# A graph network's five summing passes: separate PSUM places in place of windows, node values ahead of the pass, and f32 queries

## The chip, the cores and the metric

One core of one Trainium2 chip runs the whole kernel in one launch. The metric is the device time of that core in microseconds (us); lower is better. The kernel before takes 8,166.93 us, the median of 3 runs (8,162.49 to 8,179.8).

## The reference

Four graph layers stand one behind the other, each followed by a residual and a layer norm. There are 6,250 nodes of 128 features and 100,000 edges sorted by destination:

```python
x = _layernorm(x + _L0_gnn_ref(...))   # two GAT layers: softmax over a node's edges of leaky_relu(s[src] + d[dst])
x = _layernorm(x + _L1_gnn_ref(...))   # segment_sum(xw[src] * norm, dst)
x = _layernorm(x + _L2_gnn_ref(...))   # 8 heads: q from x[dst], k and v from a message of x[src], edge type and time
x = _layernorm(x + _L3_gnn_ref(...))   # segment_sum(m[src], dst), then a GRU cell
```

The core of each layer is `segment_sum(values of edges, dst)`: a row of 128 features for each edge, got by its source node, weighted and summed into its destination node. Layer 0 does this twice, the others once. Layer 2 needs the query row of each edge's destination as well, layer 0 the attention term `d[dst]`.

## The kernel before, in words

Nodes lie in NB = 49 blocks of 128. The edges are cut into K = 832 tiles of up to 128 edges, so that all edges of a tile go to nodes of one block. Which block that is depends on the data, so the kernel works it out on the chip (L225 to L251) and keeps it as integers for registers. U = 16 tiles make a group, 48 tiles a chunk (CHUNKS).

A summing pass goes over the 832 tiles. GpSimd (POOL in the profile) gathers 128 source rows for each tile with an indirect DMA (`gather`, L137). A 128 x 128 f32 one-hot `sel` says which edge goes to which node of the block; `selections` (L364 on) makes the one-hots once, in the first pass, stores them in the table SELD, 1 MB for 16 tiles, and loads them in all later passes. TensorE multiplies `sel` with the rows into PSUM, and VectorE adds the product to ACC in SBUF, at the place of the tile's block. There are five such passes: `attention_edges(0)`, `attention_edges(1)` (layer 0), `sum_edges` with table Yt and edge weights (layer 1), the value pass L1013 to L1032 (layer 2), which loads its rows from a table by plain DMAs, and `sum_edges` with table Mt (layer 3).

*Windows* (L402 to L458). Three or four consecutive tiles share one PSUM bank. For each pass step of 6, 8 or 12 tiles TensorE loads registers (L415) with the offset of each tile's block from the first block of its window, a bf16 zero matmul clears the bank (L437), and each tile's matmul adds at its register-held offset (L445). VectorE then adds the whole window of 390 to 512 columns to ACC in one instruction (L453), 1,250 in all.

*attention_edges* (L460 to L559). For each chunk the loop gathers 48 tiles into three row buffers (of 7, 16 tiles each). For each group it gets bf16 row one-hots, the transposed selection, from `row_selections` (L377 to L390): in pass 0 they are made from destination rows loaded by two DMAs (L385, `dlrow`, two buffers) and two VectorE compares (L386), and stored in the table RSELD (L387); in pass 1 they are loaded. One matmul with three bf16 columns per tile brings the node's attention term to the edges (L493), in pass 0 a second one brings the node's time (L496); each value is split in three bf16 parts (`by_step`, L349 on), and a reduce adds them (L501, L503). Then comes a chain of small instructions for the softmax's running maximum over the chunk (L505 to L547: transposes on TensorE, scans on VectorE), ScalarE scales the rows (L556), and the sums follow. The chain of a chunk waits for its gathers (L504), and in TensorE's order before, it begins ahead of all 48 sums of the chunk in front.

*Layer 2* has a node stage that writes a table Qt of queries, each split into three bf16 parts (L787 to L791), and then 208 steps of four tiles, whose order on TensorE is written out by hand (`part`, L841 on). A step's `rows_of` (L817 to L838) loads the query rows of each tile's block (L826, 102 KB) and 128 KB of row one-hots; `keys` (L878 to L906) multiplies messages with the key and value weights (L890, f32), and gets queries to edges with three bf16 matmuls (L892). The value pass afterwards loads 256 KB of values per four tiles (L1025) and multiplies them on GpSimd (L1027).

The scheduler of the framework keeps program order on each engine except where priorities move instructions[...].

Of the kernel before, what the change touches and what calls it, by code (L numbers as in the profile page):

```python
# [20 lines left out]
P = 128  # L21
# [14 lines left out]

WINDOWS = {3: W, 4: D}
MW = max(WINDOWS)
# [12 lines left out]
def kernel(ctx: ExitStack, tc: tile.TileContext, a: dict, out: bass.AP):  # L51
# [27 lines left out]
    RSELD = table("rseld", K // U * P, U * P, BF16)  # L79
    TYR = table("tyr", KR, P, BF16)  # L80
# [5 lines left out]
    Qt = table("qt", NP, 3 * W, BF16)  # L86
# [29 lines left out]

    OFF = const.tile([97, K + 4], I32, name="OFF")
    PLACE = {3: OFF[0:1, 0:K], 4: OFF[64:65, 0:K]}
    QOFF = OFF[32:33, 0:K]
    FIRST = {3: OFF[96:97, 0:K // 3 + 1], 4: OFF[96:97, K // 3 + 1:K // 3 + 1 + K // 4]}  # L120
    zero = const.tile([1, BANK], BF16, name="zero")
    nc.vector.memset(zero, 0.0)
# [20 lines left out]
    with tc.tile_pool(name="prep", bufs=1) as pp, tc.tile_pool(name="prepp", bufs=2, space=PSUM) as pq:  # L143
# [97 lines left out]
        for m, w in WINDOWS.items():  # L241
            n = -(-K // m)
            part = 0 if m == 3 else 64
            steps = bkrow[part:part + 1, 0:n * m].rearrange("o (w s) -> o w s", s=m)
            place = pp.tile([P, K + 4], F32, name="place", bufs=2)[part:part + 1, 0:n * m]
            nc.vector.tensor_sub(place.rearrange("o (w s) -> o w s", s=m), steps,
                                 steps[:, :, 0:1].to_broadcast([1, n, m]))
            nc.vector.tensor_scalar(PLACE[m], place[:, 0:K], float(w), None, op0=OP.mult)
            nc.vector.tensor_scalar(FIRST[m], bkrow[96:97, 0:n * m:m], float(W), None, op0=OP.mult)
# [99 lines left out]
    def by_step(keep, work, psum, rows, name):  # L349
# [7 lines left out]
        t3 = keep.tile([P, K, 3], BF16, name=f"{name}t", bufs=1)  # L357
# [4 lines left out]
        return t3  # L362
# [14 lines left out]
    def row_selections(work, k0, make=False, n=U):  # L377

        rs = work.tile([P, n * P], BF16, name="rsel", bufs=4 if n < U else 2)
        tab = RSELD[k0 // U * P:(k0 // U + 1) * P, k0 % U * P:(k0 % U + n) * P]  # L380
        if make:
            for h in range(2):
                n = U * P // 2
                row = work.tile([P, n], BF16, name="dlrow")
                nc.sync.dma_start(row, flat(DLR, k0 * P + h * n, (0, P), (1, n)))  # L385
                nc.vector.tensor_scalar(rs[:, h * n:(h + 1) * n], row, relid, None, op0=OP.is_equal)  # L386
            last = nc.sync.dma_start(tab, rs)  # L387
        else:
            last = nc.sync.dma_start(rs, tab)
        return rs, name_of(last)  # L390
# [11 lines left out]
    class Windows:  # L402
# [4 lines left out]
        def __init__(self, psum, m, banks, windows):  # L407
            self.m, self.w, self.banks, self.group = m, WINDOWS[m], banks, windows * m
            self.ring = psum.tile([P, banks, BANK], F32, name="ring")
            self.todo = []  # L410
            for t0 in range(0, NB + MW, 14):
                nc.vector.memset(ACC[:, t0:min(NB + MW, t0 + 14), :], 0.0)

        def load(self, to, engine, most):
            _, vals = nc.values_load_multi_w_load_instructions(  # L415
                to, engines=[engine], min_val=0, max_val=most,
                skip_runtime_bounds_check_because="a window has as many places as steps, and blocks are below NB")
            return vals

        def add(self, k, sel, rows, after, fade=None, kept=0):  # L420


            m, w, n = self.m, self.w, rows.shape[-1]
            if k % (U * m) == 0:
                k1 = min(K, k + U * m)
                self.to = self.load(FIRST[m][:, k // m:-(-k1 // m)], ET.DVE, (NB - 1) * W)
            if fade is not None:
                self.fades[k] = fade
            self.todo.append((k, sel, rows, after))
# [3 lines left out]
            ks = range(todo[0][0], k + 1)  # L433
            at = self.load(PLACE[m][:, ks[0]:k + 1], ET.PE, (m - 1) * w)
            wins = sorted({q // m for q in ks})
            for i, v in enumerate(reversed(wins)):
                z = nc.tensor.matmul(self.ring[:, v % self.banks, 0:m * w], zero[:, 0:P], zero[:, 0:m * w],  # L437
                                     start=True, stop=False, skip_group_check=True)
                if i == 0:
                    head = z  # L440
                    first_after(z, [a_ for t in todo for a_ in t[3]])
                else:
                    in_order(z, head)
            for q, sel, rows, _ in todo:
                last = nc.tensor.matmul(self.ring[:, q // m % self.banks, ds(at[q - ks[0]], n)], sel, rows,  # L445
                                 start=False, stop=False, skip_group_check=True)
            for v in wins:
                to = self.to[v % U]
                if v * m in self.fades:
                    a0 = ACCF[:, ds(to, kept)]  # L450
                    nc.vector.tensor_scalar(a0, a0, self.fades.pop(v * m), None, op0=OP.mult)
# [769 lines left out]
```

## Time and profile before

| | |
|---|---|
| median of 3 runs | 8,166.93 us |
| profiled execution | 8,259.27 us, span 8,257.5 us |
| mean granted TensorE clock | 0.644 |
| prep and node tables | 0 to 146 us |
| attention_edges(0) | 146 to 1,698 us |
| attention_edges(1) | 1,760 to 3,222 us |
| sum_edges of layer 1 | 3,345 to 4,588 us |
| node stage of layer 2 | to 4,686 us |
| layer 2, 208 steps | 4,686 to 6,430 us |
| value pass | 6,512 to 6,830 us |
| sum_edges of layer 3 | 6,914 to 8,134 us |

The costliest groups of instructions:

```profile
L445 PE MATMUL ring<-g,sel 128*128 128x128 f32 (+2 forms) x6656 | 1532.7, 388 | 1755.5 <-issue 1723.6
L137 POOL DMA_INDIRECT g<-g,SRCT x1664 | 1573.0, 945 | 1524.8 <-issue 836.9
L453 DVE TENSOR_TENSOR ACC<-ACC,ring 128x512 f32 (+3 forms) x1250 | 755.9, 605 | 3734.0 <-remote 2206.2
L437 PE MATMUL ring<-zero 1*128 1x408 bf16 (+1 forms) x1250 | 446.5, 449 | 963.5 <-DVE ACC L453 564.6
L890 PE MATMUL pk<-Wkv,mT 128*128 128x256 f32 x1664 | 681.7, 499 | 94.2 <-DVE qk L900 49.0
L892 PE MATMUL pq<-qb,rsel 128*128 128x136 bf16 x2496 | 331.1, 250 | 0.0
```

A line gives the source line, the engine and the operation, the tile written and the tiles read, the count, then busy time and mean ns of one, then the idle time of the engine just before such instructions and what ended most of it. An f32 matmul stands in the records twice, with two weight loads (PEld). "issue" is time in which an engine waited for nothing that the profile shows, "remote" a wait whose releaser it can't place. DVE is VectorE, ACT is ScalarE. Engine times overlap, so busy times don't add up to the span.

### The profile page before, as it was taken

How to read it: one execution, taken by the hardware profiler on the slowest of the kernel's cores; microseconds unless marked ns; L12 is line 12 of the kernel's file. 1: busy time of each engine (PE TensorE's matmuls, PEld its weight loads, DVE VectorE, ACT ScalarE, POOL GpSimd, SP SyncE). 2: the span in 40 equal slices, each digit the busy share in tenths (PEclk: the TensorE clock that was granted, in tenths of full speed). 3: DMA queues.
4: the chain of work that ended last, by engine and by line, in shares of the span. 5: the costliest groups of instructions: out<-in, count | busy, mean ns of one | idle time of the engine just before them, and what ended most of it. 6: DMA issues, size and time to landing. Idle time of an engine off the chain costs nothing. (4 is left out here: it accounts for less than half of the span.)

```text
span 8257.5 us, 75556 instructions
## 1 busy us (share of the span) xinstructions
PE 3922.3 (47%) x20491; PEld 2792.2 (34%) x20491; DVE 2618.2 (32%) x5807; ACT 1708.1 (21%) x5176; POOL 4221.7 (51%) x4384
## 2 busy tenths in 40 slices
PE   2244444433334433233333377777777693243436
PEld 1133333322223322222222244444444472132224
DVE  3122222231111114110111666566566654011115
ACT  1112121202211111222222233333333110000001
POOL 2555555435555551656666155455553373666661
PEclk8555555555555555555555688788888796555657
DMA  4333433333333322222332466666666592232321
GB/s 109 93 118 111 120 111 118 94 91 108 96 96 96 98 79 59 78 88 88 96 92 89 133 184 186 179 187 185 181 185 169 193 360 66 70 97 87 98 88 60
DMA packets 737110, 997.93 MB, mean 121 GB/s; under 512 B 151865, under 2 KB 594033, under 8 KB 703425
## 3 DMA queue, kind: packets, MB, share of 16 engines
q1 hardware_dynamic: 588090, 662.03, 25.4%
q0 software_dynamic: 146992, 331.03, 16.2%
q8 instruction: 189, 3.10, 0.2%
q14 instruction: 217, 1.77, 0.1%
q10 hardware_dynamic: 1622, 0.01, 0.0%
HBM read 824.55 MB, written 168.09 MB: 120 GB/s over the span
## 5 line engine op out<-in xcount | busy, mean ns | idle before, releaser
L445 PE MATMUL ring<-g,sel 128*128 128x128 f32 (+2 forms) x6656 | 1532.7, 388 | 1755.5 <-issue 1723.6
L137 POOL DMA_INDIRECT g<-g,SRCT x1664 | 1573.0, 945 | 1524.8 <-issue 836.9
L445 PEld LDWEIGHTS ring<-g,sel 128*128 128x128 f32 x6656 | 1336.8, 288 | 2119.7 <-issue 2119.6
L453 DVE TENSOR_TENSOR ACC<-ACC,ring 128x512 f32 (+3 forms) x1250 | 755.9, 605 | 3734.0 <-remote 2206.2
L137 POOL DMA_INDIRECT xa<-xat,SRCT x832 | 855.4, 1028 | 970.0 <-DVE z L872 582.5
L137 POOL DMA_INDIRECT g<-yt,SRCT x832 | 785.0, 943 | 589.8 <-issue 394.7
L137 POOL DMA_INDIRECT g<-mt,SRCT x832 | 785.0, 944 | 489.6 <-issue 345.5
L437 PE MATMUL ring<-zero 1*128 1x408 bf16 (+1 forms) x1250 | 446.5, 449 | 963.5 <-DVE ACC L453 564.6
L890 PE MATMUL pk<-Wkv,mT 128*128 128x256 f32 x1664 | 681.7, 499 | 94.2 <-DVE qk L900 49.0
L556 ACT ACTIVATE g<-g 128x128 f32<-128x128 f32 x1664 | 521.1, 388 | 186.1 <-issue 125.7
L575 ACT ACTIVATE g<-g,EWT 128x128 f32<-128x128 f32 x832 | 324.9, 400 | 863.9 <-DMA g<-yt,SRCT 767.6
L437 PEld LDWEIGHTS <-zero 1*128 1x128 bf16 x1250 | 106.9, 101 | 1073.6 <-issue 928.1
L890 PEld LDWEIGHTS pk<-Wkv,mT 128*128 128x128 f32 x1664 | 310.1, 232 | 132.2 <-DVE qk L900 62.1
L1027 POOL TENSOR_TENSOR vx<-v,exh 128x512 f32<-128x512 f32 x208 | 214.9, 1064 | 247.5 <-DMA v<-vt 221.2
L892 PE MATMUL pq<-qb,rsel 128*128 128x136 bf16 x2496 | 331.1, 250 | 0.0
L892 PEld LDWEIGHTS <-rsel 128*128 128x128 bf16 x2496 | 251.9, 114 | 177.6 <-issue 72.3
L898 ACT COPY kv<-pk 128x512 f32<-128x512 f32 x416 | 239.8, 600 | 348.1 <-PE pq L892 268.6
L542 ACT ACTIVATE f<-f 1x1 f32<-1x1 f32 x36 | 7.3, 202 | 1361.3 <-DVE f L541 1253.8
L860 PE MATMUL rp<-RT,oty 128*128 128x256 bf16 x832 | 259.8, 312 | 21.8 <-DMA qb<-qt 21.8
L323 ACT COPY aT<-tr 128x512 f32<-128x512 f32 (+1 forms) x13 | 7.3, 560 | 1232.2 <-PE tr L321 1232.2
L861 PE MATMUL rp<-RT,oty 64*128 64x256 bf16 x832 | 257.3, 309 | 0.0
L493 PE MATMUL pdn<-D0t,rsel 128*128 128x3 bf16 x1664 | 101.5, 167 | 321.6 <-issue 212.9
(322 smaller groups left out, 4531.4 us busy)
## 6 DMA issues: line engine op xcount, KB each, us to landing
sel<-seld SPq DMA_DIRECT2D x208, 1024.0 KB
qb<-qt SPq DMA_DIRECT2D x832, 102.0 KB
seld<-sel SPq DMA_DIRECT2D x52, 1024.0 KB
vt<-kv SPq DMA_DIRECT2D x208, 256.0 KB
v<-vt SPq DMA_DIRECT2D x208, 256.0 KB
g<-g,SRCT POOLq DMA_INDIRECT x1664
dlrow<-dlr SPq DMA_DIRECT2D x104, 256.0 KB
rseld<-rsel SPq DMA_DIRECT2D x52, 512.0 KB
```

The source lines that it names most:

```text
L137: return nc.gpsimd.indirect_dma_start(out=dst_tile, out_offset=None, in_=tab, in_offset=bass.IndirectOffsetOnAxis(ap=idx, axis=0))
L437: z = nc.tensor.matmul(self.ring[:, v % self.banks, 0:m * w], zero[:, 0:P], zero[:, 0:m * w], start=True, stop=False, skip_group_check=True)
L445: last = nc.tensor.matmul(self.ring[:, q // m % self.banks, ds(at[q - ks[0]], n)], sel, rows, start=False, stop=False, skip_group_check=True)
L453: add = nc.vector.tensor_add(a0, a0, self.ring[:, v % self.banks, 0:m * w] .rearrange("p (b w) -> p b w", w=w)[:, :, 0:n])
L556: scaled = nc.scalar.activation(g[:, q, 0:D], g[:, q, 0:D], AF.Copy, scale=g[:, q, D:D + 1])
L575: scaled = nc.scalar.activation(g[:, q, :], g[:, q, :], AF.Copy, scale=EWT[:, k0 + q:k0 + q + 1])
L860: part(nc.tensor.matmul(rp[:, q, :], oty[:, o:o + P], RT2, start=True, stop=False), after)
L861: part(nc.tensor.matmul(rp[:, q, :], oty[0:REL, o:o + P], RT3, start=False, stop=True), after)
L890: part(nc.tensor.matmul(pk[:, q - q0, :], mT[:, q, :], Wkv, start=True, stop=True), after)
L892: part(nc.tensor.matmul(pq_[:, q - q0, :], rs[:, o:o + P], qb[:, q, i, :], start=i == 0, stop=i == 2), after)
L898: free += [nc.scalar.copy(kv[:, q0:q0 + 2, :], pk), nc.scalar.copy(qbs[:, k0 % U + q0:k0 % U + q0 + 2, :], pq_[:, :, D:]), nc.vector.tenso ...
L1027: i0 = nc.gpsimd.tensor_mul(vx[:, :, 0:D].rearrange("p q (h d) -> p q h d", h=HD), v.rearrange("p q (h d) -> p q h d", h=HD), exh[:, u0:u0 ...
```

## The change: separate places, an earlier pre-pass, f32 queries

Four things change together.

- `Windows` becomes `Sums`. Each tile has a PSUM place fixed at build time, three or four to a bank. The zero matmul and TensorE's register loads go. VectorE adds each tile's product by itself, 128 to 136 columns, 4,160 adds in all, and loads the 16 places of a group of tiles into its registers at once.
- `attention_edges` brings node values to the edges for all 52 groups before the pass's first sum, with one matmul of six (pass 0) or three (pass 1) columns for each tile; in TensorE's order, a chunk's chain now begins after 36 of the 48 sums of the chunk in front.
- `sum_edges` of layer 1 also makes f32 row one-hots, 1 MB for each group, in a new table RSELF.
- Layer 2 keeps its queries in f32 (68 KB a tile's load instead of 102), loads 256 KB of f32 row one-hots a step, and does one f32 matmul for the queries of a tile. The value pass loads 1 MB of values for 16 tiles at once.

```diff
-    class Windows:
+    class Sums:
...
-            at = self.load(PLACE[m][:, ks[0]:k + 1], ET.PE, (m - 1) * w)
-            wins = sorted({q // m for q in ks})
-            for i, v in enumerate(reversed(wins)):
-                z = nc.tensor.matmul(self.ring[:, v % self.banks, 0:m * w], zero[:, 0:P], zero[:, 0:m * w],
-                                     start=True, stop=False, skip_group_check=True)
...
-            for q, sel, rows, _ in todo:
-                last = nc.tensor.matmul(self.ring[:, q // m % self.banks, ds(at[q - ks[0]], n)], sel, rows,
-                                 start=False, stop=False, skip_group_check=True)
...
+            for q, sel, rows, _, to in todo:
+                n = rows.shape[-1]
+                at = self.ring[:, q // self.m % self.banks, q % self.m * width:q % self.m * width + n]
+                mm = nc.tensor.matmul(at, sel, rows, start=True, stop=True)
...
+                a0 = ACCF[:, ds(to, n)]
+                add = nc.vector.tensor_add(a0, a0, at)
...
+            for k0 in range(0, K, U):
+                rs = row_selections(work, k0, l == 0)
+                c0 = k0 // U % slots * U * 6
+                pd = pdn[:, c0:c0 + U * nv].rearrange("p (t i) -> p t i", i=nv)
+                for q in range(U):
+                    nc.tensor.matmul(pd[:, q, :], rs[:, q * P:(q + 1) * P], DN[:, k0 + q, :], start=True, stop=True)
+                nc.vector.tensor_reduce(DE[:, k0:k0 + U], pd[:, :, 0:3], AX.X, OP.add)
+                if l == 0:
+                    nc.vector.tensor_reduce(TMT[:, k0:k0 + U], pd[:, :, 3:6], AX.X, OP.add)
...
                 sel, made_by = selections(work, k0)
+                if weighted:
+                    made_rows(work, k0, work.tile([P, U * P], F32, name="rself", bufs=2),
+                              RSELF[k0 // U * P:(k0 // U + 1) * P, :])
...
-                for i in range(3):
-                    nc.scalar.copy(q3[:, :g, i, :], qt[:, :g])
-                    if i < 2:
-                        nc.vector.tensor_sub(qt[:, :g], qt[:, :g], q3[:, :g, i, :])
-                nc.sync.dma_start(nodes(Qt)[:, t0:t0 + g, :], q3[:, :g].rearrange("p t i w -> p t (i w)"))
+                nc.sync.dma_start(nodes(Qt)[:, t0:t0 + g, :], qt[:, :g])
...
-                            for i in range(3):
-                                part(nc.tensor.matmul(pq_[:, q - q0, :], rs[:, o:o + P], qb[:, q, i, :],
-                                                      start=i == 0, stop=i == 2), after)
+                            part(nc.tensor.matmul(pq_[:, q - q0, :], rs[:, o:o + P], qb[:, q, :],
+                                                  start=True, stop=True), after)
...
+                v = work.tile([P, U, D], F32, name="v")
+                nc.sync.dma_start(v, Vt[k0 * P:(k0 + U) * P, :].rearrange("(q e) d -> e q d", e=P))
```

The new helper `made_rows` holds the loads, compares and store that `row_selections` had:

```python
def made_rows(work, k0, rs, tab):
    for h in range(2):
        n = U * P // 2
        row = work.tile([P, n], BF16, name="dlrow")
        nc.sync.dma_start(row, flat(DLR, k0 * P + h * n, (0, P), (1, n)))
        nc.vector.tensor_scalar(rs[:, h * n:(h + 1) * n], row, relid, None, op0=OP.is_equal)
    nc.sync.dma_start(tab, rs)
```

## The prediction

> **What bounds the kernel now.** I read the page's busy table and slices, then the stages as windows, then the waits, and last short windows inside the passes.
>
> ```profile
> PE 3922.3 (47%) x20491; PEld 2792.2 (34%) x20491; DVE 2618.2 (32%) x5807; ACT 1708.1 (21%) x5176; POOL 4221.7 (51%) x4384
> PE   2244444433334433233333377777777693243436
> POOL 2555555435555551656666155455553373666661
> PEclk8555555555555555555555688788888796555657
> ```
>
> No engine is busy for much over half of the span. So the limit is a hand-over, and it must be looked for stage by stage. The next view cuts the span into layer 0's two attention passes, layer 1's sums, layer 2's steps, layer 2's value pass and layer 3's sums; columns are PE, PEld, DVE, ACT, POOL busy (count), PE clock, DMA share, GB/s.
>
> ```profile
> 146.00:1698.00 1552.00, 613.75 (x3781) 470.96 (x3780) 388.26 (x841) 280.00 (x1000) 786.77 (x832) 0.54 0.36 107
> 1760.00:3222.00 1462.00, 539.34 (x2897) 406.71 (x2898) 213.73 (x648) 278.38 (x955) 783.32 (x830) 0.56 0.33 95
> 3345.00:4588.00 1243.00, 446.10 (x1874) 328.72 (x1874) 159.70 (x261) 324.88 (x832) 784.97 (x832) 0.58 0.30 90
> 4686.00:6430.00 1744.00, 1281.57 (x6775) 815.39 (x6776) 1028.60 (x2144) 635.89 (x1927) 855.39 (x832) 0.80 0.66 178
> 6512.00:6830.00 318.00, 274.61 (x1943) 225.13 (x1942) 191.56 (x356) 45.73 (x206) 214.90 (x208) 0.95 0.99 336
> 6914.00:8134.00 1220.00, 450.41 (x1872) 333.23 (x1872) 142.23 (x208) 0.00 (x0) 785.04 (x832) 0.59 0.30 90
> ```
>
> Four passes of 832 gathers take 1,220 to 1,552 us. A gather is 0.945 us and starts every 1.248 us when nothing holds it, so 832 need 1,038 us: every pass is above that. The value pass has DMA at 0.99. Layer 2's steps have PE busy 74% at clock 0.80. What holds the gather passes is in the waits:
>
> ```profile
> DVE ACC L453 <- remote: 2206.2, 135, 49.0
> PEld ring L445 <- issue: 2153.2, 1324, 5.1
> PE ring L445 <- issue: 1730.3, 1080, 4.5
> ```
>
> VectorE waits for TensorE, and TensorE's sum matmuls wait 1,730 us for nothing that the profile shows. The short windows show when: two stretches of a pass where POOL has gathered without a pause, one after a pause, and layer 1's end after its last gather.
>
> ```profile
> 168.00:284.00 116.00, 7.39 (x45) 4.71 (x45) 1.50 (x5) 0.00 (x0) 87.66 (x94) 0.50 0.30 71
> 3722.00:3752.00 30.00, 4.76 (x13) 3.43 (x13) 0.29 (x1) 8.83 (x22) 18.87 (x20) 0.55 0.17 46
> 3776.00:3789.00 13.00, 13.00 (x60) 10.11 (x59) 4.86 (x8) 3.26 (x9) 9.89 (x11) 0.59 0.62 209
> 4534.00:4584.00 50.00, 34.71 (x235) 27.62 (x234) 32.51 (x69) 0.00 (x0) 0.00 (x0) 0.84 0.41 137
> ```
>
> Under back-to-back gathers TensorE starts one record per 116/90 = 1.29 us or 30/26 = 1.15 us, weight loads and matmuls alike; after a pause, one per 13/119 = 0.11 us. The first window holds only the 3-column matmuls L493 and L496, so the slow pace isn't the work of register offsets or zero matmuls. So TensorE paces the passes, in the stretches where POOL streams; POOL then fills all row buffers, stands still some 6 us, and TensorE catches up.
>
> [...] TensorE's L415 shows 590 in layer 1. [...]
>
> **The change, part by part**, against the profiled span of 8257.5 (8259.27 for that run; the median of the runs, 8166.93, is 0.989 of it, and savings are scaled so).
>
> *No zero matmuls, no offsets on TensorE.* A tile is two weight loads and two matmuls in the records (f32); the zero matmul adds one of each per four tiles: 4.5 records a tile before, 4 after. In layer 1 POOL's cycle is 32 gathers in 45.9 us, 6 of them standing. Slow tiles cost 4.5 x 1.15 = 5.2 us, fast ones 0.49 (13 us for 119/4.5 = 26 tiles): some 26 tiles are done fast in 12.5 us, the other 6 slowly. Afterwards 0.44 and 4.6 us: 12.5/0.44 = 28.6 fast tiles per pause. With C for the cycle, 28.6 + (C - 12.5)/4.6 = (C - 6)/1.248 gives C = 52.5 us for 37.3 tiles, 1.41 us a tile instead of 1.434: 21 us a pass. The register load of TensorE goes too (104 x 0.59 = 61 us a pass); it runs beside queued matmuls, so I count at most 10 of it. Layer 1 and layer 3: -30 each. Bounds: 0 and -150 (gather pace).
>
> *One VectorE add per tile.* L453's adds took 556 ns at 390 columns and 687 at 512: 1.07 ns a column and 138 fixed, so 284 ns at 136, and six in a row took 4.43 us where durations make 4.1, so 0.05 between: 0.335 x 832 = 279 us a pass instead of about 160. A gather pass has 1,220 or more, so VectorE covers it: 0 there. Queued behind a waiting add are the chain of L501 to L547 and the one-hots; TensorE and ScalarE wait for these. In the value pass cover is gone: 279, plus the products with exh and 52 loads of 16 registers (1.1 us each, half exposed), make about 350 against 318: +30 (0 to +50). The 1 MB loads in place of four of 256 KB move the same bytes: 0.
>
> *Row one-hots for f32 queries, made in layer 1.* 52 times two loads, two is_equal with f32 out and a 1 MB store. is_equal in bf16 took 485 ns for 1024[...]. But the store waits for them, and they are behind the former group's adds, and SP issues the next sel load behind the store. DMA share is 0.30, so bytes are free; I take +25 for the coupling (0 to +60).
>
> *Pre-pass.* In attention_edges all 52 groups of 16 tiles get node values before the first sum; then 112 gathers fill the seven row buffers in 140 us and POOL stands until the first sums. Layer 0: 146 us with TensorE slow, about five groups done; then 47 groups at 4 to 5 us (two loads and a store, 1 MB in all: 3.1 us at 336 GB/s; 16 matmuls under 4 us; take 4.5): 212. Then 720 tiles, 15 chunks. A chunk takes 84 us now; its 48 tiles at layer 1's new pace need 68, and about 6 of the chain's stalls stay, because the chain of the next chunk now sits after 36 of a chunk's 48 sums and no longer ahead of all: 74. With 40 at the end: 146 + 212 + 15 x 74 + 40 = 1,508 instead of 1,552: -44. Layer 1 of the two: groups only load their one-hots (512 KB, 1.6 us) and are about 2.3 us: 146 + 46 x 2.3 + 1,110 + 40 = 1,402 instead of 1,462: -60. Bounds from 60 to 84 a chunk: -250 to +105 each.
>
> *Layer 2.* Node stage: 36 casts of 645 ns and 24 subtractions of 718 go, and alternate between two engines: -25 of 40. Steps: PE per tile at full clock is 0.43 for keys and 3 x 0.06 plus an exposed load, about 0.66; an f32 query is 2 x 0.11 and its heavier load: the same 0.66. Query loads fall from 102 to 68 KB, one-hots rise from 128 to 256 KB per four tiles: even. 0 (-20 to +66; the upper end is a load left exposed at 0.08 x 832).
>
> Sum: layers 0 -104, layer 1 -30 + 25, layer 3 -30, node stage -25, value pass +30: -134, or -132 in the median: 8,035, written 8,040.
>
> **Rivals.**
> (a) The pre-pass is not cheap, slower: POOL has nothing to do from its 112th gather to the pass's first sum, and any time a group takes more is added in full. At 8 us a group in layer 0 (load, compare, store in turn with two row buffers) and 4.6 in layer 1: 47 x 3.5 + 46 x 2.3 = 270 more, 8,305. It decides from about 1.4 us more per group in both (134/93). For it: dlrow has two buffers, and nothing in the trace shows this loop alone. Against it: loads of 256 KB and compares of 485 ns are short, and SP has no other work then.
> (b) TensorE falls below the threshold at which POOL waits for it, much faster: layers 1 and 3 at 1.248 us a tile, 1,083 each with a tail of 45: 1,243 + 1,220 - 2,166 = -297 instead of -35: 7,780; if the chunks follow, lower. For it: 0.44 us fast. Against it: without pauses TensorE stays slow at 4.6 us a tile.
> (c) The f32 query doesn't shorten but lengthens TensorE's share of a step, the part that doesn't do what it says: +66, 8,105. For it: clock 0.80 and PE 74% busy; against: VectorE 59% busy shares the step.
>
> **How the numbers follow.** Chances: forecast (7,930 to 8,140) 0.40; (a), 8,190 to 8,450, 0.31; VectorE's adds delay chain and one-hots by as much, 8,185 to 8,300, 0.08; (b), 7,550 to 7,930, 0.12; (c) 0.09, half of it within 0.2%. A measurement of this kernel can't tell less than 0.2% (16 us) from no change. Faster by over 0.2%: 0.40 + 0.12 + 0.03 = 0.55; within: 0.06; slower: 0.39. Leaving out a tenth at each end gives 7,780 to 8,400; the likeliest case alone, 7,930 to 8,140.
>
> **What would show it.** Right: layer 1 and 3 passes near 1,240 and 1,190 with no L437; a gap of POOL of about 210 and 105 us before the first sums of layer 0's passes, and chunks of 74 us; the value pass with DVE over 0.8 busy; steps still 8.4 us. Wrong: longer gaps (a), passes near 1,080 (b), steps over 8.6 us (c). The prediction fails most easily if the slow pace of TensorE changes with the kind of instruction, since its cause isn't known.

## The result, and the profile after

The changed kernel takes 8,526.81 us (median of 4 runs, 8,514.88 to 8,535.17) against 8,164.71 for the kernel before on the same chip: slower, ratio 1.044 (95% interval 1.042 to 1.046). The forecast was 8,040, faster; the range ended at 8,400.

The busy table and the slices of the changed kernel:

```profile
PE 3471.9 (41%) x17577; PEld 2793.6 (33%) x17577; DVE 3140.4 (37%) x8891; ACT 1652.6 (19%) x5137; POOL 4244.2 (50%) x4384
...
PE   2012233232232233323222347888888574133336
...
POOL 2214455543355655166666435555554263666661
...
PEclk8556555556555555555555668888888686555557
```

TensorE has 2,914 records fewer than before, VectorE 3,084 more, as the change says. What is new is at the left: POOL's third slice is at 1, PE's second at 0, and POOL's slices after it stay lower than before. The groups that answer to those of before:

```profile
L418 PE MATMUL ring<-g,sel 128*128 128x128 f32 (+2 forms) x6656 | 1504.4, 384 | 2814.7 <-issue 1816.6
...
L430 DVE TENSOR_TENSOR ACC<-ACC,ring 128x128 f32 (+3 forms) x4160 | 1200.9, 289 | 3217.8 <-remote 2136.9
...
L865 PE MATMUL pq<-qb,rsel 128*128 128x136 f32 x1664 | 404.9, 333 | 0.0
```

The zero matmuls are gone; TensorE's waits without a cause are not (1,723.6 us before, 1,816.6 now). An add takes 289 ns (284 forecast), 1,201 us in place of 756. The queries now take 1,664 records where bf16 took 2,496. By stage, with the columns that the prediction used (layer 0's two passes, layer 1, layer 2's steps, its value pass, layer 3):

```profile
150.00:1971.00 1821.00, 447.73 (x2678) 387.25 (x2678) 481.49 (x1468) 270.01 (x1000) 791.52 (x832) 0.56 0.31 91
2022.00:3547.00 1525.00, 450.40 (x2679) 394.43 (x2678) 317.86 (x1255) 264.56 (x956) 789.58 (x832) 0.56 0.32 91
3649.00:4890.00 1241.00, 355.08 (x1664) 318.79 (x1664) 303.54 (x935) 319.86 (x832) 800.43 (x832) 0.58 0.49 155
4988.00:6692.00 1704.00, 1313.54 (x6044) 958.07 (x6044) 1080.98 (x2238) 635.37 (x1933) 855.18 (x832) 0.82 0.66 181
6692.00:7078.00 386.00, 254.83 (x1685) 235.78 (x1684) 276.10 (x951) 49.24 (x214) 213.40 (x208) 0.84 0.88 287
7172.00:8389.00 1217.00, 390.31 (x1664) 326.18 (x1664) 238.37 (x832) 0.00 (x0) 785.49 (x832) 0.57 0.30 90
```

To compare like with like I cut both traces at the first gather and the last add of each pass (layer 2: first to last gather; value pass: first to last add):

| us | before | after | difference |
|---|---|---|---|
| layer 0, first pass | 1,555 | 1,821 | +266 |
| layer 0, second pass | 1,487 | 1,524 | +37 |
| layer 1 | 1,223 | 1,241 | +18 |
| node stage of layer 2 | 118 | 97 | -21 |
| layer 2's steps | 1,664 | 1,564 | -100 |
| value pass | 295 | 340 | +45 |
| layer 3 | 1,220 | 1,217 | -3 |

With small differences between the stages that makes the 256 us by which the spans differ (8,513.1 and 8,257.5).

These 256 us are not the 362 by which the two medians differ. The profiled run of the kernel before took 8,259 us, 1.1% more than the 8,161 to 8,180 of the four runs beside the changed kernel, and it is none of those four. Two later runs leave most stages as they were, on a chip where the kernel before takes 8,166: e13 (layers 1 and 3, layer 2) and e14 (layer 0). Measured against them, the changed kernel's differences are:

| us | before, from e13 and e14 | after | difference |
|---|---|---|---|
| layer 0, first pass | 1,539 | 1,821 | +282 |
| layer 0, second pass | 1,470 | 1,524 | +54 |
| layer 1 | 1,218 | 1,241 | +23 |
| node stage of layer 2 | 119 | 97 | -22 |
| layer 2's steps | 1,609 | 1,564 | -45 |
| value pass | 301 | 340 | +39 |
| layer 3 | 1,210 | 1,217 | +7 |

That is 338 us, and with some 15 between the stages it comes near the 362. The same stage differs by up to 15 us from one run to the next on such a chip (the first pass takes 1,552 in e16, whose code there is the same), so differences of that size say nothing.

The first pass of layer 0 is most of it by either table. In the two profiled runs its 266 us are a gap of POOL after the 112th gather of 289 us where 56 stood before (+233), and 40 more in the gathers behind it; its end is 10 shorter. The first four chunks behind the gap take 99 to 103 us each and the later ones 80 to 88, where the kernel before takes 81 to 86. In the second pass the gap grows from 30 to 119 us, while the gathers behind it take 1,168 us in place of 1,224.

**Chips of two kinds showed up**. On some the kernel before takes 7,028 to 7,033 us (e1 to e8, e17), on others 8,159 to 8,259 (e9 to e16, e18), and the first comparison was made on one of the latter. I call them the quick and the slow kind; all ratios are against the kernel before on the same chip. The later runs met two chips of the quick kind and four of the slow; one was met twice and was quick both times. The slow kind has two levels: 8,159 to 8,166 (the first comparison, e13 to e16, e18) and 8,250 to 8,259 (e9 to e12, and the trace of before). They differ in layer 2's steps with bf16 queries, 1,607 to 1,609 us (e13, e14) and 1,664 to 1,668 (the trace of before, e11).

The layer 1 pass of the kernel before on the slow kind, two windows side by side, then the same code on the quick kind (in e1, which leaves that pass alone):

```profile
3800.00:3840.00 40.00, 15.66 (x71) 11.65 (x71) 5.50 (x8) 10.77 (x28) 25.94 (x28) 0.63 0.31 99
3840.00:3880.00 40.00, 7.32 (x19) 4.80 (x18) 1.37 (x2) 11.50 (x29) 27.36 (x30) 0.50 0.26 74
```

```profile
3300.00:3340.00 40.00, 17.91 (x72) 14.00 (x72) 5.50 (x8) 12.41 (x33) 30.25 (x33) 0.66 0.33 106
3340.00:3380.00 40.00, 18.78 (x72) 14.37 (x72) 5.50 (x8) 12.28 (x33) 30.25 (x33) 0.62 0.32 105
```

On the quick kind TensorE does 72 matmul records in each of the two windows and POOL 33 gathers, its full pace; on the slow kind the records fall to 19 once POOL has streamed for a while. (A record is one instruction of TensorE in the trace.) The granted clock is lower there, but by a fifth only, 0.50 in place of 0.63, while the records fall to about a quarter. So the slow pace that the prediction found in the trace goes with the chip, not with the program alone.

### The profile page after: what moved, and what is told of

It reads as the page before. It is cut to its first block, busy times and chain, and to the rows that moved or that the text cites. A ratio compares the mean times of both kernels' runs of the same rounds, so it can differ in the third digit from the quotient of the medians.

```text
span 8513.1 us, 71240 instructions
## 1 busy us (share of the span) xinstructions
PE 3471.9 (41%) x17577; PEld 2793.6 (33%) x17577; DVE 3140.4 (37%) x8891; ACT 1652.6 (19%) x5137; POOL 4244.2 (50%) x4384
## 5 line engine op out<-in xcount | busy, mean ns | idle before, releaser
L418 PE MATMUL ring<-g,sel 128*128 128x128 f32 (+2 forms) x6656 | 1504.4, 384 | 2814.7 <-issue 1816.6
L430 DVE TENSOR_TENSOR ACC<-ACC,ring 128x128 f32 (+3 forms) x4160 | 1200.9, 289 | 3217.8 <-remote 2136.9
L865 PEld LDWEIGHTS pq<-qb,rsel 128*128 128x128 f32 x1664 | 406.3, 244 | 83.7
L865 PE MATMUL pq<-qb,rsel 128*128 128x136 f32 x1664 | 404.9, 333 | 0.0
L864 PEld LDWEIGHTS pk<-Wkv,mT 128*128 128x128 f32 x1664 | 335.2, 247 | 182.9 <-DVE qk L873 157.2
L456 PE MATMUL pdn<-DN,rsel 128*128 128x6 bf16 (+1 forms) x1664 | 69.1, 168 | 575.8 <-DVE rsel L375 267.9
L418 PE MATMUL ring<-vx,sel 128*128 128x136 f32 x1664 | 245.2, 312 | 107.6 <-POOL vx L1000 103.6
L873 DVE TENSOR_TENSOR qk<-kv,pq 128x256 f32<-128x256 f32 x416 | 173.5, 417 | 277.6 <-ACT qbs L872 153.7
L418 PEld LDWEIGHTS ring<-vx,sel 128*128 128x128 f32 x1664 | 232.2, 218 | 120.7 <-POOL vx L1000 119.9
L456 PEld LDWEIGHTS <-rsel 128*128 128x128 bf16 x1664 | 57.2, 105 | 591.1 <-DVE rsel L375 291.1
```

The source lines that it names most:

```text
L418: mm = nc.tensor.matmul(at, sel, rows, start=True, stop=True)
L430: add = nc.vector.tensor_add(a0, a0, at)
L864: part(nc.tensor.matmul(pk[:, q - q0, :], mT[:, q, :], Wkv, start=True, stop=True), after)
L865: part(nc.tensor.matmul(pq_[:, q - q0, :], rs[:, o:o + P], qb[:, q, :], start=True, stop=True), after)
L873: nc.vector.tensor_mul(qk[:, q0:q0 + 2, :], kv[:, q0:q0 + 2, 0:D], pq_[:, :, 0:D])]
```

## Experiments

**Each part alone, on the quick kind.** Theory 1: the pre-pass costs the time. Rival: VectorE's single adds cost it, because the chain and the one-hots are queued behind them.

e1 puts the pre-pass alone into the kernel before (`DE`, `DN` and the loop over 52 groups; windows stay):

> The kernel before with one part of the change: node values go to all edges ahead of each attention pass's sums; windows and bf16 queries stay. Theory 1 (the pre-pass costs the time): layer 0's first pass grows from 1,555 us to about 1,800, its second from 1,487 to about 1,520, all else stays, 8,430 in all. Rival (VectorE's single adds cost it, by holding up the chain and the one-hots that are queued behind them): the first pass grows by no more than 100 us, 8,250 or less.

Measured 7,445 against 7,028, ratio 1.060 (1.058 to 1.061). First pass 1,610 us in place of 1,121 (as e3 and e4 have it, which leave it alone), second 1,162 in place of 1,237. The gap is 258 us where there was none, and chunks take 67 to 79 us in place of 60. So the pre-pass does cost the time, and twice what was expected in the first pass (+489 for +245); in the second it gains 75 where a loss of 33 was expected.

e2 replaces `Windows` by `Sums` alone:

> The kernel before with one part of the change: a PSUM place of its own for each tile, one VectorE add per tile, no zero matmuls. Theory 1: layer 0's passes within 40 us of 1,555 and 1,487, the value pass 45 us longer, layer 2's steps as before, 8,200 in all. Rival: layer 0's first pass 1,650 or more, 8,300 or more.

Measured 6,969, ratio 0.992 (0.990 to 0.993): faster. First pass 1,145 (+24), second 1,122 (-115), value pass 336 (295 to 305 where it isn't changed). The rival's +100 in the first pass doesn't show. The value pass here keeps its 256 KB loads and still is 336 us long, against 347 after the whole change on the same kind of chip (e5), so most of its growth comes with the adds and not with the 1 MB loads.

e3 makes f32 queries alone:

```diff
-                            for i in range(3):
-                                part(nc.tensor.matmul(pq_[:, q - q0, :], rs[:, o:o + P], qb[:, q, i, :], ...
+                            part(nc.tensor.matmul(pq_[:, q - q0, :], rs[:, o:o + P], qb[:, q, :], ...
```

> The kernel before with one part of the change: f32 row one-hots made in layer 1, f32 queries in layer 2. If the f32 query matmul itself makes layer 2's steps shorter: steps 90 to 100 us shorter, node stage 20 shorter, layer 1's pass up to 25 longer, 8,080 in all, faster than both kernels. If the steps got shorter after the change for another reason (where ACC or a queue stands): steps within 20 us of before, 8,165.

Measured 7,099, ratio 1.010 (1.009 to 1.012), the other way: steps 1,526 us in place of 1,461, layer 1 16 longer, node stage 18 shorter. On this kind of chip f32 queries cost what the prediction's upper end had, 66. Whether by the load that it named isn't shown: in the steps TensorE's waits for VectorE's `qk` rise from 64 us (e1, bf16) to 118, and its busy time from 1,180 to 1,224.

e5 is the whole changed kernel on the same chip:

> The changed kernel once more, beside the kernel before on the same chip. The chip of the first four runs took 7,028 us for the kernel before, where the first measurement had 8,165. If the three parts add up there as they did one by one (+414, -58, +70 us) the changed kernel takes about 7,455 on such a chip, ratio 1.06; on one like that of the first measurement 8,527, ratio 1.044.

Measured 7,687, ratio 1.093 (1.092 to 1.095), +656 where the parts sum to +429. The stages say where the 227 come from: in layer 0's first pass the parts don't add (+586 against +513), and in the second pre-pass and own places each took away the same stall (chunks of 73 us become 60 with either), so that together they save only 54, where they saved 75 and 115 alone.

**What keeps the pre-pass late.** The trace of the changed kernel on VectorE, from its first measurement (start, duration, then the instruction; in brackets the idle time before it and what ended that):

```profile
177.49 0.18 DVE L478 TENSOR_TENSOR DE<-DE,g 128x16 f32<-128x16 f32 x1 [6.61 <-DMA g<-g,SRCT]
180.12 0.21 DVE L457 TENSOR_REDUCE DE<-pdn 128x16 f32<-128x48 f32 x1 [2.45 <-remote]
...
180.36 0.87 DVE L375 TENSOR_SCALAR rsel<-dlrow,relid 128x1024 bf16<-128x1024 bf16 x2
195.88 0.18 DVE L478 TENSOR_TENSOR DE<-DE,g 128x16 f32<-128x16 f32 x1 [14.65 <-DMA g<-g,SRCT]
215.83 0.21 DVE L457 TENSOR_REDUCE DE<-pdn 128x16 f32<-128x48 f32 x1 [19.77 <-remote]
```

L478 is no part of the pre-pass: it adds the gathered term of the first chunk, and the scheduler put it between the pre-pass's compares. VectorE waits there for a buffer's 16 gathers. The reduce behind it waits again, for TensorE, whose matmuls for it stand in the records 34 us earlier:

```profile
180.89 0.77 PE L456 MATMUL pdn<-DN,rsel 128*128 128x6 bf16 x16 [9.59 <-DVE TMT L459]
217.25 0.77 PE L456 MATMUL pdn<-DN,rsel 128*128 128x6 bf16 x16 [35.59 <-DVE rsel L375]
```

The reduce started (215.83 us) 34 us after the last record of these matmuls had ended (181.66); that it waited for them is read from their order, since the profile can't place the releaser, and why it came so late is not shown. Four of 52 groups were through when POOL stopped after 112 gathers. What VectorE waited for from the pass's start to its first sum, on the slow kind (first three lines) and in e1 on the quick kind (last line; L501 is what L478 is here):

```profile
DVE rsel L375 <- DMA dlrow<-dlr: 165.6, 59, 5.3
DVE DE L457 <- remote: 108.3, 5, 42.9
DVE DE L478 <- DMA g<-g,SRCT: 21.3, 2, 14.7
```

```profile
DVE DE L501 <- DMA g<-g,SRCT: 108.9, 7, 19.3
```

The numbers are us in all, times, and the longest. On the quick kind the adds of gathered terms hold the pre-pass up for 109 us; on the slow kind for 21, and there TensorE (108, by the reading above) and the loads of destination rows (166) hold it.

e6 orders these adds (and with them the chain) behind the pre-pass, whose last reduce is `made_last`:

```diff
-                    nc.vector.tensor_add(de[:, i * U:(i + 1) * U], de[:, i * U:(i + 1) * U], g[:, :, D])
+                    in_order(nc.vector.tensor_add(de[:, i * U:(i + 1) * U], de[:, i * U:(i + 1) * U], g[:, :, D]),
+                             made_last)
```

> The changed kernel with one order added: on VectorE the adds of gathered terms (with them the chain of the first two chunks) stand behind the whole pre-pass and no longer between its compares. Theory (the pre-pass is late because VectorE's queue waits in order for row buffers of 16 gathers, 20 us each): the pre-pass runs during the first 112 gathers at about 5.5 us a group, POOL's gap in layer 0's first pass falls from 258 to about 180 us where the kernel before takes 7,028, and the total by 60 to 90. Rival (the DMAs of the one-hots or TensorE set the pace beside gathers): the gap stays within 20 us.

Quick kind: 7,585, 102 less than e5; the gap 200 us in place of 263 (in the second pass 20 in place of 57). The theory holds for a quarter of the gap: 21 groups are through at the 112th gather in place of 7, and a group still takes 5.4 us. e7 adds buffers for the destination rows (`name="dlrow", bufs=4`):

> The kernel of e6 with four buffers for the destination rows in place of two. If a group of the pre-pass takes 5.5 us because its two loads wait for the compares of the group ahead: 3.5 to 4.5 us a group and a gap another 50 to 90 us shorter than in e6. If TensorE or the stores set the pace: the same as e6.

Measured 7,520, another 66 less; the gap is 121 and a group takes 4.1 us. So about 140 of the 263 us were order and two buffers; the rest is the pre-pass's own length, which no run takes apart. On the slow kind only the buffers show a gain: in e9, which has both, 4 groups are through at the 112th gather as before, and a group takes 3.8 us in place of 5.4.

**What keeps the chunks behind it long.** After the gap the first four chunks of the first pass take 99 to 106 us in e5, e6 and e7 alike, and the later ones 73. The changed kernel's VectorE, TensorE and POOL there (first measurement):

```profile
654.69 0.29 DVE L430 TENSOR_TENSOR ACC<-ACC,ring 128x131 f32 x1
654.90 0.13 DVE L516 TENSOR_SCALAR f<-f 1x1 f32<-1x1 f32 x1
673.35 0.18 DVE L478 TENSOR_TENSOR DE<-DE,g 128x16 f32<-128x16 f32 x1 [18.32 <-DMA g<-g,SRCT]
673.48 0.29 DVE L430 TENSOR_TENSOR ACC<-ACC,ring 128x131 f32 x1
```

```profile
673.83 2.99 PE L418 MATMUL ring<-g,sel 128*128 128x131 f32 x12 [13.27 <-DVE ACC L430]
```

```profile
652.02 0.94 POOL L130 DMA_INDIRECT g<-g,SRCT  x1 [12.28 <-ACT g L528]
...
685.72 0.95 POOL L130 DMA_INDIRECT g<-g,SRCT  x1 [14.03 <-ACT g L528]
```

POOL gathers the 16 tiles of a buffer, and VectorE stands 18 us at L478 until they are there. Then it does the sums' adds that were queued behind it; TensorE has waited 13 us for them, for a free PSUM place. Only then does a buffer come free and POOL goes on, 14 us later: gather and sum take turns, 33 us for 16 tiles. In the kernel before the three adds of a chunk stood together, because `de` came from a reduce at the end of the chunk (L503); made ahead of the pass, `de` is free, and the adds are spread, one between 14 to 18 sums. To reach 99 us it takes both parts of the change: with the pre-pass alone chunks take 67 to 79 us (e1) or 76 to 84 on the slow kind (e13), with single adds alone 60 to 63 (e2, not measured on the slow kind). e9 sets the three adds together again, on top of e7, behind all but the last seven of the sums' adds issued so far (`sums.added`):

```diff
+                             sums.added[-7] if sums.added else made_last)
```

> The kernel of e7 with one more order on VectorE: the three adds of gathered terms of a chunk (each waits for the gathers of one row buffer) stand together, behind all but seven of the sums' adds issued before them, and no longer one between each 16 or so. Theory (behind the pre-pass, chunks of layer 0's first pass take 73 to 99 us in place of 60 because adds that would free row buffers stand in VectorE's queue behind an add that waits for the newest gathers): the chunks take 60 to 63 us, the gathers from the 113th on 900 to 940 us in place of 1,211, and the total falls by 250 to 300, to about 7,245 where the kernel before takes 7,030. Rival (the single adds, the selections made and the chain are too much for a chunk's 60 us of VectorE or TensorE): 73 us or more a chunk stay, total within 60 us of 7,520.

This fell on the slow kind: 8,331 against 8,250, ratio 1.010 (1.008 to 1.012). The chunks there are 76 to 78 us from the first on, in place of 99 and then 81 to 82, and the gap 221 in place of 289. The buffers and the order of e7 had left the chunks alone on the quick kind, so the chunks' gain is put down to the three adds. Part of what is left has no cause that the profile shows: TensorE's sum matmuls wait 603 us for nothing in this pass. Twice more:

> The kernel of e9 once more. On the chip of e9 (kernel before 8,250 us) its chunks took 77 us[...]. On a chip where the kernel before takes 7,030: if the order of VectorE's adds was all that kept chunks at 73 to 99 us, they take 60 to 63 us here and the total is 7,245; if not, 73 and 7,500. On a chip like that of e9: 8,330 again.

8,336 against 8,259, 1.010 again.

> The kernel of e9 once more. Where the kernel before takes 7,030: chunks of 60 to 63 us and 7,245 if the order of VectorE's adds was what kept them at 73 to 99, 7,500 if not. Where it takes 8,165 to 8,260: 1.010 again.

8,311 against 8,166, 1.018 (1.016 to 1.020), with the same 77 us a chunk. This chip has the level of the first comparison, so of the 362 us that the change cost there about 217 are gone and 145 are left. Neither met the quick kind, so whether this order gives 60 us a chunk there stays open.

**The parts on the slow kind.** e13 repeats the pre-pass alone:

> The kernel of e1 once more (pre-pass alone). Where the kernel before takes 8,165 to 8,260: if the pre-pass is what the change loses there, layer 0's first pass is 230 to 300 us longer than the kernel before (a gap of POOL some 230 longer, chunks within 3 us), its second within 50, ratio 1.025 to 1.04. If the single adds share in it: ratio 1.015 or less. Where it takes 7,030: 1.060 again.

8,394 against 8,166, ratio 1.028 (1.026 to 1.030), +228. First pass 1,743 (1,539 in e14, on the same chip, which leaves it alone); gap 295. The pre-pass is the largest part of the loss there too.

> The kernel of e3 once more (f32 queries alone). Where the kernel before takes 7,030: 1.010 again, steps 66 us longer. Where it takes 8,165 to 8,250: if fewer TensorE records shorten the steps there (6 a tile for bf16 queries, 4 for f32), steps 90 to 110 us shorter than the kernel before, ratio 0.985 to 0.99; if not, 1.005 to 1.01.

8,161 against 8,259, ratio 0.989 (0.988 to 0.991): f32 queries gain 98 us here and cost 71 on the quick kind. The 98 hold for the level of 8,259, where the steps fall from 1,664 or more to 1,564; at the level of 8,166 they fall from 1,609 (e13, e14) to 1,568 (e16), by 41. With f32 queries the steps are about as long at both levels.

**A gap between gathers.** Since TensorE is slow where gathers stream (19 matmul records in 40 us in the window above), e4 puts other work between them:

```diff
+                    if weighted:
+                        nc.gpsimd.memset(pause[:, 0:D], 0.0)
+                    elif q % 8 == 7:
+                        for _ in range(4):
+                            nc.gpsimd.memset(pause, 0.0)
```

> The kernel before with idle work put between gathers on GpSimd: in layer 1's pass a small memset after each gather, in layer 3's four larger ones after each eighth (some 3 us). If TensorE's slow pace comes from gathers that follow each other without a gap, one of the two passes gets fast records (about 0.2 us a record while gathers run) and POOL no longer stands waiting for row buffers: the pass goes below 1,200 us. If it comes from the gathers' number in a stretch of time, TensorE stays slow and both passes get longer than 1,224 and 1,220, by up to 150 us.

It met the quick kind, where there is nothing to heal: layer 1 1,121 in place of 1,047, layer 3 1,346; 7,403 in a single run. e14 repeats it:

> The kernel of e4 once more (a small memset behind each gather in layer 1, four larger ones behind each eighth in layer 3). Where the kernel before takes 8,165 to 8,260: if TensorE's slow pace needs gathers without a gap, layer 1's or layer 3's pass falls below 1,200 us, or stays at 1,230 with TensorE's records no longer late; if it hangs on the share of time in which gathers run, both passes get 60 to 150 us longer. Where the kernel before takes 7,030: 1.053 again.

Slow kind: 8,296 against 8,166, ratio 1.016 (two runs). Layer 1 (0.22 us behind each gather) takes 1,224, as without. Layer 3 (3.4 us behind each eighth) takes 1,347, what it takes on the quick kind. Its waits, first in the kernel before, then in e14:

```profile
PEld ring L445 <- issue: 788.0, 475, 4.6
DVE ACC L453 <- remote: 762.6, 39, 49.0
PE ring L445 <- issue: 692.6, 378, 4.5
```

```profile
DVE ACC L453 <- PE ring L445: 1204.0, 104, 19.0
PEld L437 <- DMA g<-mt,SRCT: 889.8, 104, 14.7
...
PEld ring L445 <- issue: 87.1, 104, 1.1
PE ring L445 <- issue: 0.3, 1, 0.3
```

With that gap TensorE no longer waits without a cause (692.6 us become 0.3); it waits for gathers. The gap costs POOL more than it gives back (1,347 us against 1,220). Shorter ones:

> The kernel of e16 with memsets of 0.86 us on GpSimd between gathers: two behind each eighth gather in layer 0's first pass, one behind each eighth in its second and in layer 3, one behind each sixteenth in layer 1. Where the kernel before takes 8,165 to 8,260: if a gap lets TensorE catch up, the passes come near gathers plus gaps, 1,121 + 182, 1,121 + 90, 1,047 + 90 and 1,047 + 45: about 1,305, 1,215, 1,140 and 1,095 in place of 1,552, 1,435, 1,218 and 1,232; any one that doesn't move shows a gap too short. If only the number of gathers in a stretch counts: each within 30 us of e16's or longer. Where it takes 7,030: every pass longer by its gaps, 7,350 in all.

Quick kind again, 7,361 (7,350 expected there). The last run holds the same question and that of e9:

> The kernel of e9 (pre-pass, own places, f32 queries; the chain of the first chunks behind the pre-pass; a chunk's three adds of gathered terms together) with memsets of 0.86 us on GpSimd in the later gather passes: two behind each eighth gather in layer 0's second pass, one behind each sixteenth in layer 1, one behind each eighth in layer 3. Where the kernel before takes 7,030: layer 0's first pass has chunks of 60 to 63 us if the order of the adds was the cause, 73 and more if not; the other passes are longer by their gaps. Where it takes 8,165 to 8,260: chunks of 77 us again in the first pass; if gaps let TensorE catch up, the second pass's chunks fall from 77 to some 71 us, layer 1 from 1,240 to about 1,110, layer 3 from 1,220 to about 1,140; where one stays, its gap is too short.

Slow kind: 8,226 against 8,159, ratio 1.009 (1.007 to 1.010), where e15, the same without gaps on another chip of that level, had 1.018. One memset of 0.86 us behind each eighth gather (layer 3: 1,216, in e15 1,218) or sixteenth (layer 1: 1,225, in e15 1,240) changes little. Two behind each eighth, 1.7 us, change the first part of layer 0's second pass. There TensorE brings node values to the edges while the first 112 gathers run; first without gaps (e15), then with them (e18):

```profile
1823.00:1966.00 143.00, 4.76 (x98) 3.33 (x98) 9.01 (x15) 0.00 (x0) 109.18 (x112) 0.50 0.32 81
```

```profile
1815.00:1978.00 163.00, 24.52 (x642) 21.39 (x643) 16.17 (x50) 0.00 (x0) 132.50 (x139) 0.50 0.60 178
```

TensorE does 642 matmul records in place of 98, and 39 of the 52 groups are through at the 112th gather in place of 5. The gap shrinks from 118 to 44 us and the pass from 1,504 to 1,450. The gathers behind the gap still take 1,145 us, in e15 1,148, so the sums there are no quicker, although the sum matmuls' waits without a cause fall from 568 to 351 us. So 1.7 us behind each eighth gather is enough for the small matmuls of the pre-pass, 0.86 us is not for sums (layer 3), and 3.4 us is (e14). The chip doesn't explain it: in the first pass, which has no gaps in e18, 4 groups are through at the 112th gather and chunks take 77 us, as in e9 and e15.

**Versions that beat both.** e8 takes own places where they pay by e2 (layer 0's second pass, layers 1 and 3), windows elsewhere, no pre-pass, bf16 queries:

> The kernel before with tiles' own PSUM places in layer 0's second pass, layer 1 and layer 3, windows in layer 0's first pass and in the value pass, no pre-pass and bf16 queries. From the stages of e2: second pass 115 us shorter than before, value pass as before: 6,915 where the kernel before takes 7,028, ratio 0.984, faster than both. On a chip with a slow TensorE beside gathers: no more than 0.99.

Quick kind: 6,912 against 7,031, ratio 0.983 (0.982 to 0.985). All four gather passes stand at 832 x 1.247 us = 1,038 and a tail (the second of layer 0 takes 1,121 in all); POOL's slices show it:

```profile
PE 3592.8 (52%) x19797; PEld 2762.2 (40%) x19797; DVE 2887.7 (42%) x7607; ACT 1685.4 (24%) x5176; POOL 4232.1 (61%) x4384
...
POOL 1777776277777517777753555555550645777771
```

> The kernel of e8 once more (own PSUM places in layer 0's second pass, layers 1 and 3; windows elsewhere; no pre-pass; bf16 queries). Where the kernel before takes 7,030: 0.983 again. Where it takes 8,165 to 8,250, if what the change saves there is TensorE's records: each of the three passes 20 to 60 us shorter and a ratio of 0.98 to 0.99; if the chain's hops set the pace there: within 0.5% of before.

Slow kind: 8,229 against 8,259, ratio 0.997 (0.996 to 0.998), within the 0.5% that was expected if the chain's hops set the pace. But that doesn't follow from it: layers 1 and 3 have no chain, and with 1,228 and 1,223 us they don't get shorter either (1,223 and 1,220 with windows). Fewer records hardly helped in these two passes. e16 adds f32 queries:

> The kernel of e8 (own places in three passes, windows in layer 0's first pass and the value pass, no pre-pass) with f32 queries. If the parts add up: 6,980 where the kernel before takes 7,030 (ratio 0.993), 8,130 where it takes 8,260 (0.985): faster than both kernels on both kinds of chip. If they don't: no better than e8 there (0.983 and 0.997).

Slow kind: 8,107 against 8,166, ratio 0.994 (0.992 to 0.996). That is less than the sum of the parts, 0.985, mostly because the 98 us of f32 queries in that sum came from the other level; the steps gain 41 here. On the quick kind it wasn't run alone (e17 holds it, with gaps). All these gains are below 2%.

## Why the prediction was wrong, point by point

- **The pre-pass is the step that failed**, in three terms. It gave layer 0's first pass 1,508 us; measured 1,821, and a forecast of -44 became +266 to +282.
  1. *The gap.* The 113th gather was forecast 146 + 212 = 358 us after the pass begins, measured 433. Four groups were done when POOL stopped, about the five that were forecast. Behind them a group takes 5.4 to 5.7 us, not 4.5, because two buffers of destination rows hold it back (166 us of waits for `dlrow`; 4.1 us with four buffers in e7, 3.8 in e9), and some 16 us pass from the last group to the 113th gather. That adds of gathered terms stand between the compares costs time on the quick kind (e6, 102 us), little here (21 us of waits).
  2. *The chunks*, the largest term. Forecast were 15 of 74 us, 1,110 in all; measured 1,289, or 86 each. The prediction said that what waits behind an add is covered, since a pass has 1,220 us; it priced VectorE by its busy time alone. What counts there is what stands in front in the queue: adds for the newest gathers ahead of sums that free buffers (e9: 99 to 77). Even the 77 of e9 are not the 74.
  3. *The end.* Forecast 40 us after the last gather, measured 99, and in the trace of before it was 110 already.
- **Layer 0's second pass** was forecast at 1,402 us, -60; measured 1,524, +37 to +54. The gap was nearly right (252 us to the 113th gather, measured 263), the chunks took 1,168 us in place of 1,110, and the end 93 in place of 40. The end is a slip of reading in both passes: the trace of before had 110 and 93. With these two, the prediction's own sum was -134 + 70 + 53 = -11, no change, and its "faster" rested on that slip.
- **No zero matmuls, fewer records:** -30 each forecast for layers 1 and 3, -3 to +7 for layer 3 measured. The sum took the pace as so much per record; 4 records in place of 4.5 did nothing there (e11: layer 3 1,223, total 0.3% less). The model of fast and slow stretches was fitted to one cycle of one trace. On the quick kind own places saved 115 us in layer 0's second pass (e2), which it didn't foresee.
- **f32 queries:** 0 forecast (-20 to +66). On the quick kind +66 in the steps, the upper end. On the slow kind -41 to -45 at the level of the first comparison and -100 at the other, both outside. Where the granted clock is 1.00, a tile's keys and queries follow each other on TensorE every 0.66 us before (5,013 to 5,014 us of the trace) and after (5,303 to 5,305), as forecast. TensorE has 5,614 matmul records in most of the steps (1,562 us) in place of 6,423 (1,660 us), and I read the gain as fewer late records; no run shows that by itself.
- **VectorE's adds in the value pass:** +30 forecast (0 to +50), +39 to +45 measured. The adds bring it (e2), but the sign that was named, VectorE busy over 0.8, did not come: it is 252.7 of 337 us in e2 and 251.1 of 340 after the change, and DMA is at 0.99 in e2 as before. How the adds lengthen the pass is not shown.
- **One-hots in layer 1:** +25 forecast together with -30; measured +16 alone on the quick kind (e3) and +18 to +23 in all. A compare of 1,024 columns with f32 out took 0.75 us (L375, the median of 104), with bf16 out 0.485.
- **Node stage:** -25 forecast, -21 to -22 measured.
- **Rival (a)** named the right place and the two buffers. It put 8 us a group where 5.4 to 5.7 was measured, and its price (8,305) missed the chunks behind the gap. The smaller chance that VectorE's adds delay the chain had the right engine; what it lacked is that the adds do so only together with the pre-pass.
- **What the trace couldn't tell** is that the slow pace goes with the chip. On the quick kind the change costs 9.3%, not 4.4%: there POOL has no gap in the first pass of the kernel before and its chunks take 60 us, the pace of the gathers (48 x 1.247 us), so all that the pre-pass adds is seen.

What stays open: the cause of TensorE's late records on the slow kind, and of its two levels; the chunks of e9 on the quick kind; the rest of the pre-pass's gap.

## What to carry to other kernels

When a step is moved ahead, look at what each engine's queue then holds between its instructions. Here VectorE stood 18 us at one add for data just asked for, and behind it stood the work that would have freed the buffers for the next. A wait that hid a fixed order (here `de` from the chunk's own reduce) can be what kept that order good. Before a pace in one trace is built into a sum, see whether it holds on a second chip, and check the model on a stretch that it wasn't fitted to.

## What was not expected of the hardware

The same program took 7,028 to 7,033 us on some chips and 8,159 to 8,259 on others, 16 to 18% more. On the latter TensorE's records come late above all while GpSimd gathers back to back (one per 1.247 us): 19 matmul records in 40 us of layer 1's pass, where the quick kind has 72. 3.4 us of other work on GpSimd behind each eighth gather ends it for sums (692.6 us of waits without a cause become 0.3), and 0.86 us doesn't (685.1 us of them in e18); 1.7 us lifts small bf16 matmuls from 98 records to 642 beside 112 gathers. In the changed kernel's pre-pass the records of 16 small matmuls ended 34 us before the reduce behind them started. Layer 2's steps, where gathers don't stream, are longer on these chips too (1,607 to 1,668 us with bf16 queries, in place of 1,461), so streaming gathers are not the whole difference.
